# A two-layer graph network on one core: product order in layer 0, start-up, block sums and last stages changed

## The chip, the core and the metric

The kernel runs on one core of a Trainium2 chip. A core has five engines that run their own instruction queues beside each other: TensorE (PE: matrix products, written to the eight banks of PSUM), VectorE (DVE), ScalarE (ACT), GpSimd (POOL) and SyncE (SP, which here only issues DMA transfers). They wait for each other through semaphores. The metric is the device time of one execution in microseconds (us).

## What is computed

`x` has 64 graphs of 256 nodes with 512 features, `adj` is one 256x256 matrix for all of them. All is float32.

```python
def _L0_gnn_ref(x, adj, weight, bias):
    y = jnp.einsum('nm,bmd->bnd', adj, x)
    return jnp.einsum('bnd,do->bno', y, weight) + bias

def _L1_gnn_ref(x, adj, Wq, bq, Wk, bk, Wv, bv, Wo, bo):      # 8 heads of 64
    q, k, v = (x @ Wq + bq), (x @ Wk + bk), (x @ Wv + bv)     # split into heads
    scores = jnp.einsum('bqhd,bkhd->bhqk', q, k) / jnp.sqrt(jnp.float32(HD))
    scores = scores + (1.0 - adj)[None, None, :, :] * -1000000000.0
    attn = jax.nn.softmax(scores, axis=-1)
    out = jnp.einsum('bhqk,bkhd->bqhd', attn, v).reshape(b, n, d)
    return out @ Wo + bo

h = jnp.maximum(_layernorm(x, axis=-1), 0.0)
x = x + _L0_gnn_ref(h, adj, L0_gnn_weight, L0_gnn_bias)
h = jnp.maximum(_layernorm(x, axis=-1), 0.0)
x = x + _L1_gnn_ref(h, adj, ...)
```

## The kernel before

The 64 graphs go through in 32 groups (g) of two. Each large product is cut into 2x2 blocks and computed with seven block products in place of eight (a form of Strassen's method). For this, sums of blocks are made of both factors: `s1` to `s4` of a weight, `t1` to `t4` of the data. For layer 1 of the later groups the blocks are cut once more; the small sums this needs are made by `block_sums` (of weights), `block_hidden` and `block_outputs` (of data).

The order of all instructions is the order in which the program text issues them, on each engine for itself. A list with delays helps: `after(n, f)` puts work off by n ticks, and `tick()` (L322) runs what is due. The pieces of the twice cut products are issued by strings of tokens (`QK`, `VO`, `V1`, `O1`, `OL`, from L213 on), one `|` for each tick.

**Start.** `load(0)` issues the DMAs of x's first group on SyncE's queue, eight blocks; `adj` comes through ScalarE's queue. `turn_adjacency` (L374) reorders adj on ScalarE, transposes it on TensorE and copies it out. `first_ready` normalizes group 0: VectorE makes the moments, GpSimd the power -1/2, VectorE the shift `nb`, ScalarE the normalized `h`. `first_adjacency` multiplies by adj (tiles `py`). `ready(1, ...)` does the moments and `h` for group 1, whose power `rs` is made by GpSimd and whose shift `nb` by VectorE.

**Layer 0.** For each group `project` (L508) multiplies the result yT by the layer's weight in seven products of eight matmul passes each; the calls are `layer0(g, seeds)`. There are three PSUM banks: `pa` (w_a in the profile), `pb` (w_b) and `pc` (w_c). The order, with the bank and the data operand, is a11 (pa, b11), a12 (pb, b21), s2 (pa, t2), s3 (pc, t3), s1 (pa, t1), a22 (pc, t4), s4 (pa, b22). Products into pa, and a22 into pc, add to what stands there: between them VectorE reads the intermediate value (`x<-w_a`, `x<-w_c`, L821) and adds it to x. Between the products of group g the loop sets those of `adjacency(g + 1)` (tiles `py`), 0 to 2 behind each, by the tuple `(1, 1, 2, 2, 1, 0, 0)`. The t sums are made by GpSimd (L498), t1 and t2 first and t3 and t4 some ticks later. VectorE has in one queue the reads of the seven products, the moments (L42, L43) of the group just finished and of the group g + 2, the reads of the adjacency products and the 32x32 transposes of `turn` (L1006), which wait for ScalarE's `h` (L1000).

**Layer 1.** For each group and each half of the heads (qd), `score` makes the logits and ScalarE the exponentials, `key_sum` (L1209, GpSimd) adds pairs of keys, `attend` multiplies by ones (`pden`) and v (`pav`), `invert` makes the reciprocal, and `divide` writes oT. `score` subtracts the row `top` on GpSimd or VectorE in the blocks whose PSUM was not seeded. Between them stand the projections of the next group. `block_sums` of q and k are done at g = 0, of v at g = 1, of o at g = 2; for each letter of a product four sums of 128x128 are queued, on VectorE for B, F and G (not for o), else on GpSimd.

**End.** After the last scores, part of the output projection of group 30 (`O1`) is issued, then `attend(31, 1)`, the rest of `O1`, and the output projection of group 31 (`OL`). The blocks of x that are complete are written out.

Of the kernel before, what the change touches and what calls it, by code (L numbers as in the profile page):

```python
# [11 lines left out]
ALU = mybir.AluOpType  # L12
# [60 lines left out]
def general_path(tc, x, adj, w0, b0, wq, bq, wk, bk, wv, bv, wo, bo, out):  # L73
# [159 lines left out]
    "vBj x vDc vBk vDd | vEc vDe vEd vDf vCg vp11 vCi vCh vCj vEf vCk vEe vm11 vDg | vDi vDj vEf2 vDk vDh vEi vCl "  # L233
    "vEj vEg vm10 vEk | vEl0 vEl1 vEh vEl2 ")
O1 = (
    "oCi oAz oCj oCk oA0 oBz oA1 x oFa | oA2 oA3 oFb x oCa oEa oFc | oFd oB0 oEb oFe op00 oB1 x oFf oCl0 oEc oFi "
    "| oFj oCb oFg oCl1 oFk oEd oFh oCc x oCd oFl oB2 oB3 | op10 oDa op11 oG0 oDb oG1 oCe oCf | oG2 oEe oG3 oEf "
    "oDc om11 oDd oEg oCg | oDe oDi oDf oDj oEi oEh oDk oCh oEj oEk om10 oDg | oEl oDh ")
OL = (
    "oAz oCi oCj oCk oA0 oBz oA1 oA2 | oA3 oFa op00 oCa oFb oB0 oCb | oEa oCl0 oFc oFd oCc oEb oFe oCd oCl1 oFi "  # L240
    "oCe oFf oCf oFj | oFg oFk oEc oEd oFh oCg oFl oDa oB1 op10 | oB2 oB3 oDb oCh oG0 oEe op11 oDc oDd | oG1 oEf "
    "oDe oG2 oDf oG3 oDi | om11 oEg oDj oDk oEh oDg oEi om10 oEj oEk oDh | oEl ")


@with_exitstack
def kernel(
# [92 lines left out]
    def blocks_of(xt, i, k):  # L339
        return xt[32 * i:32 * i + 32, k * NT:(k + 1) * NT, :]  # L340

    def load(g):
        X[g] = xpool.tile([P, T, D], F32, tag=f"x{g % 4}", name=f"x_{g}")
        for k in range(GB):
            for i in range(NI):
                nc.sync.dma_start(blocks_of(X[g], i, k), by_block(x[g * GB + k], i))

    def quarter(xt, i, k):

# [155 lines left out]
                nc.tensor.matmul(ps[:, m, :], lhs, rhs, start=(start and m + c == 0), stop=(c == 1),  # L505
                                 skip_group_check=True)

    def project(s, halves, by_token, name, place, first, done=None, seeds=()):  # L508

        def put(ps, i, k):
            first(place(i, k), ps, i)

        def more(ps, i, k):
            o = place(i, k)
            add(o, ps, o)

        def complete(i, k):  # L520
            if done:
# [12 lines left out]
        product(pa, s, "s2", halves, "t2", by_token, start=False, stop=False)  # L534
        put(pa, 1, 0)
        yield
        pc = pc or bank([P, 2, N], f"{name}c")
        product(pc, s, "s3", halves, "t3", by_token, start=not seeds, stop=False)
        put(pc, 1, 1)
        yield  # L540
        product(pa, s, "s1", halves, "t1", by_token, start=False, stop=False)
        more(pa, 1, 1)
        complete(1, 1)
        yield
        product(pc, s, "a22", halves, "t4", by_token, start=False)
        more(pc, 1, 0)
        give(pc)
        complete(1, 0)
        yield
        product(pa, s, "s4", halves, "b22", by_token, start=False)  # L550
        put(pa, 0, 1)
        give(pa)
        complete(0, 1)
        yield
# [10 lines left out]
    def block_sums(n):  # L565

        todo = []
        for x in SMALL[n]:
            w = W[n][BLOCKS[x][0]]
            def part(i, j):  # L570
                return w[:, j, i * P:(i + 1) * P]
            s1, s2, s4 = (spare.pop(0) for _ in range(3))
            W2[n, x] = dict(a11=part(0, 0), a12=part(0, 1), a22=part(1, 1), s1=s1, s2=s2, s3=part(1, 0), s4=s4)
            eng = nc.vector if x in "BFG" and n != "o" else nc.gpsimd
            for o, p, q, op in ((s1, part(1, 0), part(1, 1), ALU.add), (s2, s1, part(0, 0), ALU.subtract),
                                (part(1, 0), part(0, 0), part(1, 0), ALU.subtract), (s4, part(0, 1), s2, ALU.subtract)):
                todo.append((eng.tensor_tensor, o, p, q, op))
        return todo
# [272 lines left out]
    def ready(g, moments_at, scales_at, relus_at, batches=1):  # L851


        xt = X[g]
        mv = small.tile([P, T, 2], F32, tag="mv", name=f"mv0_{g}")
        n = T // batches
        h = []

        def scales(i):
            part, name = mv[:, i * n:(i + 1) * n, :], f"0_{g}_{i}"  # L860
            if g == 1:
                rs = power(nc, small, mhalf, part, name)
                h.append((rs, shift(nc, small, part, rs, name)))
            else:
                h.append(norm_scales(nc, small, mhalf, part, name))
            if i == 0:
                H0[g] = act.tile([P, T, D], F32, tag="h", name=f"h_{g}", bufs=2)

        def relu(t):
            rs, nb = h[t // n]  # L870
            nc.scalar.activation(H0[g][:, t, :], xt[:, t, :], AF.Relu,  # L871
                                 bias=nb[:, t % n:t % n + 1], scale=rs[:, t % n:t % n + 1])

        for t in range(T):
# [115 lines left out]
    def layer0(g, seeds):  # L990
# [37 lines left out]
                if len(done) == 4:  # L1028
                    after(wait + 2, leave_hidden)

        yield from project(W["0"], halves, True, f"w_{g}", lambda i, k: quarter(xt, i, k), add_to, finished, seeds)


    H1T, HH, HO = {}, {}, {}
# [33 lines left out]
    def block_outputs(g, step):  # L1068
        x = OT[g][:, 2:4, :].rearrange("p c (k n j) -> p k c n j", k=GB, j=P)
        t = KEPT["o" if g < NG - 1 else "h3"]  # L1070
        both = Blocks(x, t[:, 0:2])
        last = Blocks(HO[g].all[:, 1:3].rearrange("p t c (n j) -> p t c n j", j=P), t[:, 2:4])
        if g == NG - 1:
            both.sums(nc.gpsimd)
            last.sums(nc.gpsimd)
        else:
            after(step, last.sums, nc.gpsimd)
            after(step, both.sums, nc.gpsimd)
        O2[g] = {"C": both.one(0), "E": both.one(1), "F": last.one(0), "D": last.one(1)}
# [68 lines left out]
    def score_seeds(g, qd):  # L1148
        return {cb: score_bank(g, qd, *cb, seed=maskT_f, times=1.0 / SCALE) for cb in ((0, 0), (0, 1))}

    def score(g, qd, sums=(5, 6, 7, 8), exps=(3, 4, 5, 8), masked=None, top_at=0):


        pair = [act.tile([P, GB, 2 * NT, N], F32, tag="h", name=f"a_{g}_{qd}_{c}", bufs=2) for c in range(2)]
# [4 lines left out]
        for c in range(2):  # L1159
            for b in range(GB):  # L1160
# [18 lines left out]
                    give(ps[j])  # L1179
                if not seen:  # L1180
                    if (g == NG - 1 or (g, qd) == (0, 0)) and b == 1:
                        after(2, lambda a: nc.vector.tensor_tensor(a, a, top_b, op=ALU.subtract), a)
                    elif top_at:
                        after(top_at, lambda a: nc.gpsimd.tensor_tensor(a, a, top_b, op=ALU.subtract), a)
                    else:
                        nc.gpsimd.tensor_tensor(a, a, top_b, op=ALU.subtract)  # L1186
                if exps is None:
# [23 lines left out]
    def attend(g, qd):  # L1211
# [49 lines left out]
        def divide():  # L1261
            for f in range(2):
                nc.vector.tensor_tensor(OT[g][:, 2 * qd + f, :], po[f], rden, op=ALU.mult)  # L1263
                give(po[f])
            if final:
                after(2, note)
            late = 6 if (g, qd) == (NG - 2, 1) else 4 if (g, qd) == (NG - 1, 0) else 0
            which = ("t3", "t2", "t4") if qd else ("t1",)
            if late:
                after(late, HO[g].sums, nc.gpsimd, which)  # L1270
            else:
                HO[g].sums(nc.vector if final else nc.gpsimd, which)
            if qd and g >= FIRST2:
                block_outputs(g, late + 1)

# [16 lines left out]
    for i in range(7):  # L1292
        side[20 + i].append((lambda: next(mask_steps, None),))

    turn_adjacency()
    first_ready()
    load(1)
    ready(1, (4, 4, 4, 4), (8,), (9, 9, 9, 9))
# [14 lines left out]
    for g in range(NG - 1):  # L1313
# [3 lines left out]
        if g + 2 < NG:  # L1317
            ready(g + 2, (1, 1, 1, 1), (1,), (3, 3, 3, 3) if g else (4, 4, 4, 4))
            after(4 if g else 5, feature_sums, g + 2)
            after(5 if g else 6, last_feature_sum, g + 2)  # L1320
        weighted, turned = layer0(g, seeds), adjacency(g + 1)
        for i, n in enumerate((0, 0, 1, 2, 2, 2, 0) if g == 0 else (1, 1, 2, 2, 1, 0, 0)):
            next(weighted)
# [28 lines left out]
    for g in range(NG):  # L1352
# [2 lines left out]
        if g + 2 < NG:  # L1355
            load_hidden(g + 2)
        if g == NG - 1:
            score(g, 1, (2, 3, 5, 4), (1, 2, 4, 3), top_at=3)
        else:
            score(g, 1, exps=None if g + 1 >= FIRST2 else (3, 4, 5, 8))  # L1360
        tick()
        if g == 0:
            for pool, n, tag, used in ((const, 4 * DC, "w0_sb", None), (const, 4, "w0_s1", None), (const, 4, "w0_s2", None),
# [7 lines left out]
                    first = 3 * used[1]  # L1371
                    KEPT[used[0]] = t[:, 0:first].rearrange("p (t q) j -> p t q j", q=3)
                spare.extend(t[:, i, :] for i in range(first, n))
        for n, at in (("q", 7), ("k", 16)) if g == 0 else (("v", 3),) if g == 1 else (("o", 2),) if g == 2 else ():
            for i, work in enumerate(block_sums(n)):
                after(at + i // (2 if n == "v" else 4), *work)
        if g + 1 < FIRST2:
            for which in queries_keys(g + 1):
                run(plain(g + 1, *which))
# [5 lines left out]
            run(follow(steps, QK))  # L1385
        else:
            last = follow(quartered_outputs(g - 1), O1)
            run(last, 4)
        attend(g, 1)
        if g + 1 < NG:  # L1390
            score(g + 1, 0, (5, 6, 7, 8) if g + 1 < NG - 1 else (1, 1, 1, 1), None if g + 1 >= FIRST2 else (3, 4, 5, 8))
# [79 lines left out]
```

## Time and profile before

| what | us |
|---|---|
| median of 3 runs | 2619.58 (2619.09 to 2621.03) |
| the profiled execution | 2618.1 |
| its span, first to last instruction | 2616.3 |
| TensorE busy | 2587.3 |
| stretch 0 to 52 (start, first two groups): TensorE busy | 39.89 |
| stretch 52 to 540 (layer 0): TensorE busy | 487.16 |
| stretch 540 to 1000: TensorE busy | 456.40 |
| stretch 1000 to 2480: TensorE busy | 1480.00 |
| stretch 2570 to 2616.3 (end): TensorE busy | 33.95 |

In the profile, PE is a matmul and PEld the load of its weights. A float32 matmul shows as two passes. A row of the timeline has the start, the length from the first start to the last end of the merged instructions, the engine and line, and out<-in by the program's names. The brackets at the end give the idle time of the engine before it and what ended it. Passes overlap: eight of 256 columns that follow each other take 1.73 us from start to start although each is listed with 379 ns. In the list of waits the columns are the total, the number and the longest.

### The profile page before, as it was taken

The numbers are of one execution on the slowest core, as the hardware profiler recorded it, in microseconds if no ns is written. First come the engines' busy times: TensorE is split into PE (matmuls) and PEld (weight loads), VectorE is DVE, ScalarE is ACT, GpSimd is POOL, SyncE is SP. The second block draws the span as 40 slices with busy tenths as digits, with TensorE's granted clock in tenths as the row PEclk, the third lists the DMA queues.
The fourth block names the chain that finished last, engine by engine and source line by source line (L and its number), as shares of the span: only waits on it lengthen the run. The fifth ranks groups of instructions, "written<-read, shape, count | busy, mean of one in ns | idle before, by whom it ended". The sixth has DMA issues, their size and how long they took to land.

```text
span 2616.3 us, 57383 instructions
## 1 busy us (share of the span) xinstructions
PE 2587.3 (99%) x21876; PEld 2304.1 (88%) x21876; DVE 1910.3 (73%) x4165; ACT 1379.8 (53%) x3198; POOL 2077.2 (79%) x2259
## 2 busy tenths in 40 slices
PE   8999999999999999999999999999999999999998
PEld 7999899998888888888888888888888888888886
DVE  6888788875576677777776777777777777777776
ACT  4545454543455555555555555555555555555553
POOL 6788887774788888888877888888888888887785
PEclk9999999999999999999999999999999999999999
DMA  5776666664111222211111111111122221111101
GB/s 149 198 193 182 171 165 184 161 163 112 33 50 49 64 63 66 54 50 50 50 49 50 49 50 50 50 50 49 49 62 64 65 56 50 50 49 50 50 34 50
DMA packets 281111, 211.40 MB, mean 81 GB/s; under 512 B 145920, under 2 KB 212992, under 8 KB 280832
## 3 DMA queue, kind: packets, MB, share of 16 engines
q1 hardware_dynamic: 280224, 207.02, 29.9%
q8 instruction: 175, 2.87, 0.4%
q14 instruction: 104, 0.85, 0.1%
q10 hardware_dynamic: 608, 0.66, 0.1%
HBM read 106.96 MB, written 100.66 MB: 79 GB/s over the span
## 4 chain that ended last, share of the span: by engine, by line
PE 88%; POOL 5%; DVE 4%; DMA 2%; issue 1%; SPq 1%; ACT 1%; DVEq 0%; ACTq 0%; POOLq 0%
PE sc L1166 9%; PE pav L1225 8%; PE o_pa L662 4%; PE pden L1218 2%; PE v_pa L648 2%; PE q_pa L648 2%; PE k_pa L648 2%; PE v_pa L662 2%; PE o_pc L662 2%; PE q_pa L662 2%; PE k_pa L662 2%; PE o_pa L648 2%; PE v_pc L648 1%; PE q_pc L648 1%; PE k_pc L648 1%; DVE st L42 1%
## 5 line engine op out<-in xcount | busy, mean ns | idle before, releaser
L1174 DVE SCALAR_TENSOR_TENSOR a<-sc,top 128x512 f32<-128x512 f32 x256 | 159.0, 684 | 262.1 <-PE sc L1166 262.1
L1209 POOL TENSOR_TENSOR as<-a 128x512 f32<-128x512 f32 x256 | 320.4, 1281 | 7.8 <-ACT a L1202 6.2
L1186 POOL TENSOR_TENSOR a<-a,top 128x1024 f32<-128x1024 f32 x124 | 291.1, 2370 | 36.7 <-DVE a L1177 36.7
L1242 POOL TENSOR_TENSOR as<-as 128x512 f32<-128x512 f32 x64 | 80.9, 1264 | 275.1 <-ACT as L1241 264.3
L1202 ACT ACTIVATE a<-a 128x1024 f32<-128x1024 f32 x256 | 271.9, 1063 | 23.5 <-POOL a L1186 11.9
L1166 PE MATMUL sc<-q,k 64*128 64x256 f32 x2048 | 239.5, 383 | 0.0
L1166 PEld LDWEIGHTS sc<-q,k 64*128 64x128 f32 x2048 | 196.7, 187 | 43.3 <-issue 25.4
L1225 PE MATMUL pav<-a,v 128*32 128x256 f32 x4096 | 233.6, 379 | 0.0
L1225 PEld LDWEIGHTS pav<-a,v 128*32 128x32 f32 x4096 | 133.6, 110 | 87.8
L1232 ACT ACTIVATE as<-pden 128x512 f32<-128x512 f32 x64 | 38.3, 598 | 283.3 <-PE pden L1218 283.3
L42 DVE BATCH_NORM_STATS2 st<-x 128x6 f32<-128x512 f32 x256 | 173.2, 677 | 10.8 <-DMA x<-in_x_dram 8.0
L1177 DVE SCALAR_TENSOR_TENSOR a<-sc,maskT 128x512 f32<-128x512 f32 x256 | 158.3, 681 | 0.0
L306 ACT ACTIVATE sc<-maskT 128x512 f32<-128x512 f32 x256 | 137.5, 590 | 0.0
L1000 ACT ACTIVATE h<-x,nb,rs 128x512 f32<-128x512 f32 x128 | 97.2, 808 | 65.7 <-POOL nb L54 63.9
L871 ACT ACTIVATE h<-x,nb,rs 128x512 f32<-128x512 f32 x124 | 90.8, 803 | 65.4 <-POOL nb L54 62.3
L934 POOL TENSOR_TENSOR hs<-h 128x512 f32<-128x512 f32 x31 | 39.4, 1270 | 72.9 <-ACT h L871 71.1
L821 DVE TENSOR_TENSOR x<-o_pa,x 128x512 f32<-128x512 f32 (+1 forms) x121 | 82.4, 682 | 9.0 <-PE o_pa L662 5.2
L1263 DVE TENSOR_TENSOR oT<-pav,as 128x512 f32<-128x512 f32 x128 | 82.1, 683 | 9.2 <-POOL as L1244 9.2
L1087 ACT ACTIVATE q<-q_pa,bq_c 128x256 f32<-128x256 f32 (+1 forms) x150 | 61.7, 456 | 50.1 <-PE q_pa L648 37.6
L597 POOL TENSOR_TENSOR spare<-h1T,spare 128x128 f32<-128x128 f32 x180 | 82.2, 456 | 7.0
L1244 POOL TENSOR_TENSOR as<-as 128x512 f32<-128x512 f32 x64 | 81.0, 1265 | 5.4
L498 POOL TENSOR_TENSOR t_y<-yT,t_y 128x512 f32<-128x512 f32 (+1 forms) x65 | 82.2, 1265 | 3.4 <-ACT yT L906 1.0
(1637 smaller groups left out, 8741.1 us busy)
## 6 DMA issues: line engine op xcount, KB each, us to landing
x<-in_x_dram SPq DMA_DIRECT2D x256, 128.0 KB, 3.0
residual<-x SPq DMA_DIRECT2D x256, 128.0 KB, 2.5
hidden<-r SPq DMA_DIRECT2D x128, 256.0 KB, 4.5
h1T<-hidden SPq DMA_DIRECT2D x64, 512.0 KB, 7.4
x<-residual SPq DMA_DIRECT2D x32, 1024.0 KB, 7.9
out_dram<-x SPq DMA_DIRECT2D x62, 512.0 KB, 4.1
w_sb<-in_L_gnn_weight_dram SPq DMA_DIRECT2D x1, 1024.0 KB, 8.3
wq_sb<-in_L_gnn_Wq_dram SPq DMA_DIRECT2D x1, 1024.0 KB, 7.3
```

The source lines that it names most:

```text
L42: nc.vector.bn_stats(st, src)
L306: nc.scalar.mul(t, seed, times)
L648: nc.tensor.matmul(o[:, 0, :], lhs, rhs, start=bool(fresh), stop=True, skip_group_check=True)
L662: nc.tensor.matmul(t[:, m, :], lhs, rhs, start=starts, stop=True, skip_group_check=True)
L1000: nc.scalar.activation(h1[:, k * NT + t, :], xt[:, k * NT + t, :], AF.Relu, bias=nb[:, t:t + 1], scale=rs[:, t:t + 1])
L1166: nc.tensor.matmul(ps[j][:, kt * N:(kt + 1) * N], k[j * HD:(j + 1) * HD, c, kt * P:(kt + 1) * P], q[j * HD:(j + 1) * HD, c, :], start=(kt ...
L1174: nc.vector.scalar_tensor_tensor(o, ps[j].rearrange("p (k n) -> p k n", k=NT), SCALE, top_b[:, 0:NT, :], op0=ALU.mult, op1=ALU.subtract)
L1177: nc.vector.scalar_tensor_tensor(o.rearrange("p k n -> p (k n)"), ps[j], SCALE, maskT_f, op0=ALU.mult, op1=ALU.add)
L1186: nc.gpsimd.tensor_tensor(a, a, top_b, op=ALU.subtract)
L1202: nc.scalar.activation(a, a, AF.Exp)
L1209: nc.gpsimd.tensor_tensor(AS[c, b], a4[:, :, 0, :], a4[:, :, 1, :], op=ALU.add)
L1225: nc.tensor.matmul(po[f][h * 32:(h + 1) * 32, b * N:(b + 1) * N], v[:, k, h * HD + f * 32:h * HD + f * 32 + 32], A[h // 2, b][:, (h % 2) * ...
```

## The change

It has these parts:

- `project` gets `spaced`: in layer 0 the product s1 t1 (into pa) is issued ahead of s3 t3 (into pc). The value of pa is then the first to be added to the (1,1) quarter of x, that of pc the second.
- `keep_busy`: 11 matmuls of the identity by itself, 128x128, ahead of adj's transposes on TensorE, and 8 behind them, into a bank that is given back without being read.
- two of the first four DMA blocks of x are issued on ScalarE's queue, ahead of adj's.
- `ready` makes the shift `nb` of group 1 when the first `h` is issued, and no longer together with the power; `last_feature_sum(2)` comes one tick later.
- the `block_sums` of v are all on GpSimd, from tick 9 on, eight to a tick; those of o start at tick 9 and not at 2.
- last stages: new strings `O1` and `OL`; six and not four groups of `O1` ahead of `attend(31, 1)`; the subtractions of `top` in `score(31, 1)` are no longer put off; the final sums of the data (t2, then t3, t4) on VectorE in another order; the block sums for `OL` in another order and two in separate halves.

```diff
-    def project(s, halves, by_token, name, place, first, done=None, seeds=()):
+    def project(s, halves, by_token, name, place, first, done=None, seeds=(), spaced=False):
...
-        pc = pc or bank([P, 2, N], f"{name}c")
-        product(pc, s, "s3", halves, "t3", by_token, start=not seeds, stop=False)
-        put(pc, 1, 1)
-        yield
-        product(pa, s, "s1", halves, "t1", by_token, start=False, stop=False)
-        more(pa, 1, 1)
-        complete(1, 1)
-        yield
+        def third(then):
+            nonlocal pc
+            pc = pc or bank([P, 2, N], f"{name}c")
+            product(pc, s, "s3", halves, "t3", by_token, start=not seeds, stop=False)
+            then(pc, 1, 1)
+
+        def fifth(then):
+            product(pa, s, "s1", halves, "t1", by_token, start=False, stop=False)
+            then(pa, 1, 1)
+
+        for part, then in ((fifth, put), (third, more)) if spaced else ((third, put), (fifth, more)):
+            part(then)
+            if then is more:
+                complete(1, 1)
+            yield
...
-        yield from project(W["0"], halves, True, f"w_{g}", lambda i, k: quarter(xt, i, k), add_to, finished, seeds)
+        yield from project(W["0"], halves, True, f"w_{g}", lambda i, k: quarter(xt, i, k), add_to, finished, seeds, spaced=True)
...
-                nc.sync.dma_start(blocks_of(X[g], i, k), by_block(x[g * GB + k], i))
+                queue = nc.scalar if (g, k) == (0, 0) and i % 2 else nc.sync
+                queue.dma_start(blocks_of(X[g], i, k), by_block(x[g * GB + k], i))
...
+    idle = bank([P, NT, N], "idle")
+
+    def keep_busy(n):
+
+        for _ in range(n):
+            nc.tensor.matmul(idle[:, 0, 0:P], ident, ident, start=True, stop=True)
+
+    keep_busy(11)
     turn_adjacency()
+    keep_busy(8)
+    give(idle, False)
...
             if g == 1:
-                rs = power(nc, small, mhalf, part, name)
-                h.append((rs, shift(nc, small, part, rs, name)))
+                h.append((power(nc, small, mhalf, part, name), None))
...
         def relu(t):
             rs, nb = h[t // n]
+            if nb is None:
+                nb = shift(nc, small, mv[:, t // n * n:(t // n + 1) * n, :], rs, f"0_{g}_{t // n}")
+                h[t // n] = rs, nb
...
-            eng = nc.vector if x in "BFG" and n != "o" else nc.gpsimd
+            eng = nc.vector if x in "BFG" and n in "qk" else nc.gpsimd
...
-        for n, at in (("q", 7), ("k", 16)) if g == 0 else (("v", 3),) if g == 1 else (("o", 2),) if g == 2 else ():
+        for n, at in (("q", 7), ("k", 16)) if g == 0 else (("v", 9),) if g == 1 else (("o", 9),) if g == 2 else ():
             for i, work in enumerate(block_sums(n)):
-                after(at + i // (2 if n == "v" else 4), *work)
+                after(at + i // (8 if n == "v" else 4), *work)
...
-            after(5 if g else 6, last_feature_sum, g + 2)
+            after(5 if g else 7, last_feature_sum, g + 2)
...
         if g == NG - 1:
-            both.sums(nc.gpsimd)
-            last.sums(nc.gpsimd)
+            for part in (last.one(0), last.one(1), both):
+                part.sums(nc.gpsimd)
...
-                        after(2, lambda a: nc.vector.tensor_tensor(a, a, top_b, op=ALU.subtract), a)
-                    elif top_at:
-                        after(top_at, lambda a: nc.gpsimd.tensor_tensor(a, a, top_b, op=ALU.subtract), a)
+                        after(0 if qd else 2, lambda a: nc.vector.tensor_tensor(a, a, top_b, op=ALU.subtract), a)
...
-            if late:
+            if final:
+                HO[g].sums(nc.vector, ("t2", "t3", "t4"))
+            elif late:
...
-            score(g, 1, (2, 3, 5, 4), (1, 2, 4, 3), top_at=3)
+            score(g, 1, (2, 3, 5, 4), (1, 2, 4, 3))
...
-            run(last, 4)
+            run(last, 6)
...
 O1 = (
-    "oCi oAz oCj oCk oA0 oBz oA1 x oFa | oA2 oA3 oFb x oCa oEa oFc | oFd oB0 oEb oFe op00 oB1 x oFf oCl0 oEc oFi "
+    "oAz oFa oFb oA0 oBz oFc oA1 x | oA2 oDa oCa x oEa oFd oA3 oFe oB0 | oFf oB1 x oB2 oB3 oFg op00 | oCb oEb oFi "
...
 OL = (
-    "oAz oCi oCj oCk oA0 oBz oA1 oA2 | oA3 oFa op00 oCa oFb oB0 oCb | oEa oCl0 oFc oFd oCc oEb oFe oCd oCl1 oFi "
+    "oAz oBz oA0 oA1 oA2 | oEa oA3 oFa oCi oFb oB0 oEb oB1 op00 | oB2 oFc oFd oB3 oFe oCj op11 oFf | oFi oFg oFj "
...
```

More of the change, by code (lines that the diff above doesn't have):

```diff
@@ L235 @@
 O1 = (
-    "oCi oAz oCj oCk oA0 oBz oA1 x oFa | oA2 oA3 oFb x oCa oEa oFc | oFd oB0 oEb oFe op00 oB1 x oFf oCl0 oEc oFi "
-    "| oFj oCb oFg oCl1 oFk oEd oFh oCc x oCd oFl oB2 oB3 | op10 oDa op11 oG0 oDb oG1 oCe oCf | oG2 oEe oG3 oEf "
-    "oDc om11 oDd oEg oCg | oDe oDi oDf oDj oEi oEh oDk oCh oEj oEk om10 oDg | oEl oDh ")
+    "oAz oFa oFb oA0 oBz oFc oA1 x | oA2 oDa oCa x oEa oFd oA3 oFe oB0 | oFf oB1 x oB2 oB3 oFg op00 | oCb oEb oFi "
+    "op11 oFj oFk oEc oFh x oEd | oCc oFl oCd oDi op10 oDj oDk oCi oEe oCj om10 oG0 | oG1 oEf oDb oG2 oCe oCf oG3 "
+    "oDc om11 | oDd oEg oCk oDe oCg oDf oEi oEj oCh oEk oEh oDg | oEl oDh oCl0 oCl1 ")
 OL = (
-    "oAz oCi oCj oCk oA0 oBz oA1 oA2 | oA3 oFa op00 oCa oFb oB0 oCb | oEa oCl0 oFc oFd oCc oEb oFe oCd oCl1 oFi "
-    "oCe oFf oCf oFj | oFg oFk oEc oEd oFh oCg oFl oDa oB1 op10 | oB2 oB3 oDb oCh oG0 oEe op11 oDc oDd | oG1 oEf "
-    "oDe oG2 oDf oG3 oDi | om11 oEg oDj oDk oEh oDg oEi om10 oEj oEk oDh | oEl ")
+    "oAz oBz oA0 oA1 oA2 | oEa oA3 oFa oCi oFb oB0 oEb oB1 op00 | oB2 oFc oFd oB3 oFe oCj op11 oFf | oFi oFg oFj "
+    "oFk oDi oFh oDj oFl oDk oCa oDa op10 | oDb oCb oG0 om10 oDc oDd oG1 oDe | oDf oCk oCc oCl0 oCd oG2 oCl1 oG3 "
+    "oCe oCf oDg oEc om11 | oEd oCg oDh oEi oEe oEj oEf oEk oCh oEg oEl | oEh ")
 @with_exitstack
@@ L1149, in score_seeds, with score @@
         return {cb: score_bank(g, qd, *cb, seed=maskT_f, times=1.0 / SCALE) for cb in ((0, 0), (0, 1))}
-    def score(g, qd, sums=(5, 6, 7, 8), exps=(3, 4, 5, 8), masked=None, top_at=0):
+    def score(g, qd, sums=(5, 6, 7, 8), exps=(3, 4, 5, 8), masked=None):
         pair = [act.tile([P, GB, 2 * NT, N], F32, tag="h", name=f"a_{g}_{qd}_{c}", bufs=2) for c in range(2)]
@@ L1268, in divide @@
             which = ("t3", "t2", "t4") if qd else ("t1",)
-            if late:
+            if final:
+                HO[g].sums(nc.vector, ("t2", "t3", "t4"))
+            elif late:
                 after(late, HO[g].sums, nc.gpsimd, which)
             else:
-                HO[g].sums(nc.vector if final else nc.gpsimd, which)
+                HO[g].sums(nc.gpsimd, which)
             if qd and g >= FIRST2:
```

## The prediction

> **What bounds the kernel now.** I read the page's busy shares first, then the idle waits of TensorE, then the timeline of each stretch that the diff touches. The busy shares make TensorE (PE) the bound: a change can gain only where it waits or runs slowly, and it loses where it makes TensorE wait.
>
> ```profile
> PE 2587.3 (99%) x21876; PEld 2304.1 (88%) x21876; DVE 1910.3 (73%) x4165; ACT 1379.8 (53%) x3198; POOL 2077.2 (79%) x2259
> ```
>
> The list of TensorE's waits has three places: the start, one wait in the middle, the end.
>
> ```profile
> PE pa L382 <- ACT adj_p L377: 6.5, 1, 6.5
> PE o_Fs L648 <- ACT o_F L685: 2.9, 1, 2.9
> PE py L897 <- ACT h L842: 2.8, 1, 2.8
> PE o_Es L648 <- DVE x L821: 2.8, 1, 2.8
> PE w_0a L505 <- DVE x L821: 1.7, 1, 1.7
> PE q_pb L648 <- DVE q_F L821: 1.4, 1, 1.4
> PE pden L1218 <- POOL as L1209: 1.4, 2, 0.8
> ```
>
> Layer 0 is not in that list but is what the first edit reorders in all 32 groups. One round of it, by the timeline (start, length, engine and line, out<-in):
>
> ```profile
> 207.51 1.89 PE L505 MATMUL w_9a<-w_s,yT 128*128 128x256 f32 x8
> 207.71 0.69 DVE L821 TENSOR_TENSOR x<-w_9c,x 128x512 f32<-128x512 f32 x1 [1.93 <-PE w_9c L505]
> ...
> 214.47 1.89 PE L505 MATMUL w_10a<-w_s,t_y 128*128 128x256 f32 x8
> ...
> 216.91 1.28 POOL L498 TENSOR_TENSOR yT<-yT 128x512 f32<-128x512 f32 x1
> 216.92 1.29 DVE L1006 STREAM_TRANSPOSE r<-h 128x512 f32<-128x512 f32 x2
> 217.09 1.06 PE L950 MATMUL py_11b<-adjT,h 128*128 128x128 f32 x8
> 218.14 0.65 DVE L821 TENSOR_TENSOR x<-w_10a,x 128x512 f32<-128x512 f32 x1
> ```
>
> See two things. The product s3 t3 (w_10c) starts at 218.25, when GpSimd has written t3 (216.91 + 1.28 = 218.19), about 0.25 late. And VectorE's read of bank pa after s2 t2, the last row, begins only at 218.14 and ends at 218.79, although its product ended at 216.2. VectorE is working off a queue. The windows view, from the read of the a22 product (207.71) to the end of that row, has it (columns: PE, PEld, DVE, ACT, POOL busy, clock, DMA share, GB/s):
>
> ```profile
> 207.71:218.79 11.08, 10.99 (x67) 9.93 (x66) 10.66 (x24) 4.07 (x7) 10.29 (x15) 1.00 0.75 203
> 341.01:352.10 11.09, 11.09 (x68) 10.20 (x67) 10.67 (x24) 4.65 (x7) 10.15 (x15) 1.00 0.57 153
> ```
>
> VectorE is busy for 10.66 of 11.08 us, and for the same length in a round where t3 is not late.
>
> **What the Trainium skill says.** "PSUM — Partial Sum Buffer", section "Engine vs sequencer instructions": VectorE's queue is strict first in, first out, and matmuls start in program order; the rows above agree, the finished s2 product waits its turn behind two transposes. The same page's section on bank collisions wants accesses of two engines to a bank guarded by semaphores, so the next product into pa must wait for that read. "SBUF — State Buffer", section "SBUF: two separate sides": VectorE with two SBUF inputs and GpSimd lock each other out of a shared port; the trace agrees, a 128x128 VectorE sum that takes 0.28 elsewhere took 1.72 and 2.33 from 732.69 on, beside a GpSimd pass. "TensorE: Matmul & The Clock Gate", Part 1: the array starts at half clock until a window of about 3.4 us was busy; the trace agrees, 10 passes of 128x256 in 4.42 us from 10.48, 22 in 4.40 us from 15.30.
>
> **Part 1: s1 t1 ahead of s3 t3.** Nothing is added or removed; only the order of products and of VectorE's reads changes. Before, pa is written by s2 and then by s1 3.5 us of TensorE work later (s3 and two adjacency products lie between). After, s1 follows s2 with only two adjacency products between, and those end before VectorE has read pa.
>
> Take round 10, with the end of the a22 product (207.51) as zero. TensorE is ready for the third product after s4, a11, adjacency, a12, adjacency, s2 (4 x 1.73 + 2 x 0.89 = 8.69) and two more adjacency products (1.79): 10.48. VectorE has read s2 out of pa at 218.79 - 207.51 = 11.28. From VectorE's end to a waiting product pass 0.14 us (the wait of w_31a: 605.99 to 606.13), and its first pass is 0.08 longer. So s1 starts at 11.42. In round 17 the read ends at 11.28 too, so this is VectorE's own work and not a wait that moves with TensorE. From s1 on: 1.73 + 0.08, two adjacency products 1.79, s3 1.73, one adjacency product 0.89. Then a22 goes into pc, which s3 has just filled: VectorE's read starts 0.20 after the product, lasts 0.69, plus 0.14, against 0.89 of cover: 0.14 late, and 0.08 for the first pass. Then a22 itself, 1.73. Round: 11.42 + 1.81 + 1.79 + 1.73 + 0.89 + 0.22 + 1.73 = 19.59. Before it was 18.70 where t3 was late (207.51 to 226.21) and 18.34 where it was not (322.47 to 340.81). The t3 wait is gone, and VectorE's read is late in its place.
>
> From the end of a22 in group 1 (58.62) to that in group 30 (600.45) there are 29 rounds, 541.8 us. After: 29 x 19.59 = 568.1, plus what the longer VectorE queues of some rounds (bias and mask steps: their reads of s2 ended 0.3 to 1.7 later than 11.28) and one round held by TensorE's own bias product (2.5) cost above 11.28: 8.6, the shorter last round taken off. Sum 576.7: +34.9. I take it whole because nothing in VectorE's queue moves forward. Bounds: with 0.06 us for the signal, no longer first passes and half of the extra steps hidden, +21; with all at their largest, +38.
>
> Group 1: s1 is not late there (its read ends 0.8 before TensorE is ready), a22 is: +0.2. Group 31 runs without adjacency products: s1 waits 1.1 where s3 waited 0.5, and a22 directly behind s3 waits 0.20 + 0.69 + 0.14 + 0.08 = 1.1: +1.7.
>
> **Part 2: the start.** TensorE's py products start at 10.48 and run 11 passes at half clock. 19 more small matmuls before and behind the adjacency transposes warm it; they cover TensorE's idle time and cost nothing as long as they end before h. Two of x's first four blocks go ahead of adj on ScalarE's queue: x is complete earlier (VectorE's first row started at 7.41), but adj, which ended ScalarE's wait at 5.98, is issued two DMAs later (4 issues took 1.85, so some 0.9), and ScalarE must turn adj before it makes h. I put py at 10.0, and 32 passes at 0.216 end at 16.9 instead of 19.8: 2.9. The shift of nb_1 behind x<-w_0a in VectorE's queue takes away the wait for GpSimd's power (23.16), so s2 starts at about 21.4 instead of 25.72: 4.3 ahead. What is late next: h_1, moved back with nb_1, costs the adjacency product about 0.9, and s1 of group 0 now waits for VectorE's sums of w, four moments of x_2 (26.58 to 29.8, 3.4 us, whose data come when the DMAs let them) and two reads: s1 at 27.7, s3 at 31.3, where the fourth product stood at 32.32. Gain left: 1.0. Bounds: 0, if x_2 lands no earlier, to 3.5.
>
> **Part 3: block sums of v and o.** 12 small sums of v leave VectorE; GpSimd takes 12 x 0.46 = 5.5 us more, behind the key sums, in a stretch where it was idle for 7.9 of 10 us (750 to 760). The port lock-out that held q_F until 736.71 goes with them: 1.4 and its followers 0.7 (738.5, 751.9), and the key sum that held pden at 818 comes ahead of the sums of o: 0.8. Gain 2.9 (bounds 1.5 and 3.2).
>
> **Part 4: the last stages.**
>
> ```profile
> 2570.00:2616.30 46.30, 33.95 (x252) 28.14 (x249) 29.62 (x65) 10.18 (x21) 21.54 (x23) 0.89 0.13 47
> ...
> 2578.71 0.79 PE L648 MATMUL o_Fs<-spare 128*128 128x128 f32 x2 [2.85 <-ACT o_F L685]
> ...
> 2584.54 0.84 PE L1218 MATMUL pden<-as,ones 128*32 128x256 f32 x10 [0.77 <-POOL as L1209]
> ...
> 2594.45 0.49 PE L648 MATMUL o_Es<-spare,spare 128*128 128x128 f32 x2 [2.81 <-DVE x L821]
> ```
>
> Each long wait also drops the clock (0.89). The new order gives TensorE 9.6 us of products before attend (20 of 128 columns at 0.22, 12 of 256 at 0.43) instead of 7.0, and GpSimd subtracts top first instead of idling 1.49 at 2575: its last key sum ends near 2582.7 instead of 2584.5, about when TensorE is there. Behind attend (4.3 plus 0.3 to the next read) are left 8 small O1 products, 1.8, and OL's 28 small and 12 large ones, 11.6, with about 0.8 of waits: 2582.7 + 4.6 + 14.2 = 2601.5, and 1 us more for waits I haven't found, 2602.4 against 2610.4. Gain 8.0; bounds 4 (one long wait stays) and 10.5.
>
> **The sum.** Against the profiled run (2618.1; span 2616.3): -1.0 + 0.2 + 34.9 + 1.7 - 2.9 - 8.0 = +24.9, so 2643.0. The median before is 1.5 above that run, so the forecast for a median is 2644.5.
>
> **The rivals.** (a) 72%: as summed, 2637 to 2650. (b) 12%: the read is late, but the signal is short, first passes are not longer and the extra steps are hidden, +21 for the loop; with the same other parts 2631. For it: GpSimd's signal for t3 took only 0.06. (c) 10%, faster: s1's wait for pa is covered. Then the t3 waits go (with the first pass 0.1 to 0.36 a round, 6.0 in all), no new ones come, and the sum is -1.0 - 6.0 - 2.9 - 8.0 = -17.9: 2601.7. It decides if VectorE reads s2 within 10.3 us of a22's end; 11.28 in round after round speaks against it. (d) 6%: the loop as in (a) and the end gains nothing because another wait follows the first: 2652.
>
> **The numbers.** The measurement can tell 0.2%, 5.2 us. Only (c) lies below that line: faster 10%; about 2% fall within it, slower 88%. The range 2630 to 2652 takes in (a), (b) and most of (d).
>
> **What would show it.** In layer 0: a round of 19.6, w_a<-w_s,t_y twice in a row with a wait of about 0.9 for DVE x before the second, none for t_y, and a short one before the second w_c. The start: py in passes of 0.216 from the first. The middle: no wait of q_pb. The end: clock near 1.00. I am wrong if the list of waits has no new row of w against DVE x.

## The result, and the profile after

The changed kernel takes 2642.5 us (median of 4 runs, 2641.07 to 2643.14) against 2619.66 before: 1.0086 times, with a 95% interval of 1.0068 to 1.0103. It is slower by 22.8 us; the forecast was 2644.5, range 2630 to 2652. The profiled execution has a span of 2640.4 us, 24.1 more than before.

TensorE is still the bound, but it now waits, as the page's busy shares show:

```profile
PE 2599.5 (98%) x21914; PEld 2310.3 (87%) x21914; DVE 1906.0 (72%) x4153; ACT 1385.9 (52%) x3198; POOL 2085.1 (79%) x2275
```

TensorE is busy for 12.2 us more than before (8.6 of them the small matmuls of the start, in which it had stood idle), and the rest of the 24.1 is idle time. The list of TensorE's waits in the changed kernel (line, releaser, then total, times, longest) shows where:

```profile
PE pa L383 <- ACT adj_p L378: 2.6, 1, 2.6
PE o_pb L656 <- DVE x L829: 1.9, 1, 1.9
PE w_0a L506 <- DVE x L829: 1.9, 1, 1.9
PE w_25a L506 <- DVE x L829: 1.6, 1, 1.6
...
PE o_pa L656 <- DVE x L829: 1.1, 1, 1.1
...
PE py_1a L960 <- ACT h L881: 0.7, 1, 0.7
...
PE w_10a L506 <- DVE x L829: 0.7, 1, 0.7
```

The row of w_10a stands there for nearly every group: w against DVE x, the row that the prediction asked for. Before, only groups 0 and 31 had it. The long waits of the middle and the end, `q_pb`, `pden`, `o_Fs` (2.9) and `o_Es`, are gone, and `o_pb` is new.

One round of the changed kernel by its timeline (start, length, engine and line, out<-in):

```profile
217.22 0.69 DVE L829 TENSOR_TENSOR x<-w_9c,x 128x512 f32<-128x512 f32 x1 [2.15 <-PE w_9c L506]
...
223.98 1.89 PE L506 MATMUL w_10a<-w_s,t_y 128*128 128x256 f32 x8
...
226.42 1.29 DVE L1016 STREAM_TRANSPOSE r<-h 128x512 f32<-128x512 f32 x2
...
226.60 1.06 PE L960 MATMUL py_11b<-adjT,h 128*128 128x128 f32 x8
...
227.64 0.65 DVE L829 TENSOR_TENSOR x<-w_10a,x 128x512 f32<-128x512 f32 x1
...
228.34 1.99 PE L506 MATMUL w_10a<-w_s,t_y 128*128 128x256 f32 x8 [0.69 <-DVE x L829]
...
234.73 1.97 PE L506 MATMUL w_10c<-w_sb,t_y 128*128 128x256 f32 x8
```

The second w_10a<-w_s,t_y is s1. After the adjacency product py_11b TensorE could go on at 227.49 (226.60, and 0.89 for its eight passes from start to start); VectorE ends its read of pa at 228.29, and s1 starts at 228.34. The last row is a22 (1.97 long, where 1.89 is a product that didn't wait): it starts 0.15 late, for VectorE's read of s3. The windows view of the same stretch, from the read of the a22 product to the end of the read of s2 (columns: PE, PEld, DVE, ACT, POOL busy, clock, DMA share, GB/s):

```profile
217.22:228.29 11.07, 10.43 (x64) 9.43 (x62) 10.66 (x24) 4.72 (x8) 9.39 (x17) 1.00 0.54 140
```

VectorE is busy for 10.66 of 11.07, to the hundredth what it was before. Nothing in its queue has moved; TensorE now wants the read sooner than VectorE comes to it.

Where the 24.1 us come from, by the starts of the same products in both traces:

| stretch | forecast | measured |
|---|---|---|
| start, to the first product of group 1 (41.08 to 43.74) | -1.0 | +2.7 |
| group 1 | +0.2 | -0.4 |
| 29 rounds, end of a22 in group 1 to that in group 30 (541.8 to 571.0) | +34.9 | +29.1 |
| group 31 | +1.7 | +1.6 |
| middle, up to the last stages | -2.9 | -4.1 |
| last stages | -8.0 | -4.8 |
| sum | +24.9 | +24.1 |

The sum is right within 1 us, and partly by luck: the start and the end were forecast 6.9 too good, the loop, the middle and the groups 1 and 31 7.7 too bad.

### The profile page after: what moved, and what is told of

Its sections match the earlier page's. It is cut to its first block, busy times and chain, and to the rows that moved or that the text cites. A ratio compares the mean times of both kernels' runs of the same rounds, so it can differ in the third digit from the quotient of the medians.

```text
span 2640.4 us, 57496 instructions
## 1 busy us (share of the span) xinstructions
PE 2599.5 (98%) x21914; PEld 2310.3 (87%) x21914; DVE 1906.0 (72%) x4153; ACT 1385.9 (52%) x3198; POOL 2085.1 (79%) x2275
## 4 chain that ended last, share of the span: by engine, by line
PE 86%; DVE 9%; DMA 2%; issue 1%; POOL 1%; SPq 1%; ACT 0%; DVEq 0%; POOLq 0%; ACTq 0%
PE sc L1176 9%; PE pav L1233 8%; DVE st L42 4%; PE o_pa L670 4%; DVE x L829 2%; PE pden L1226 2%; PE q_pa L656 2%; PE k_pa L656 2%; PE v_pa L656 2%; PE v_pa L670 2%; PE k_pa L670 2%; PE q_pa L670 2%; PE o_pc L670 2%; PE q_pc L656 2%; PE k_pc L656 2%; PE v_pc L656 1%
## 5 line engine op out<-in xcount | busy, mean ns | idle before, releaser
L1210 ACT ACTIVATE a<-a 128x1024 f32<-128x1024 f32 x256 | 272.4, 1065 | 18.6 <-POOL a L1194 15.7
```

Source lines behind the costliest of these rows:

```text
L1210: nc.scalar.activation(a, a, AF.Exp)
```

## The experiments

Each was timed beside runs of the kernel before on the same chip; the differences below are against those.

**1 to 4: the change taken apart.** The swap alone is the diff's edits of `project` and of its call in `layer0`, in the kernel before.

> The kernel before with s1 t1 ahead of s3 t3 and nothing else. Theory (the swap makes TensorE wait for VectorE's read of pa): rounds of 19.5 in the loop, +29 there, +1.6 in group 31, -0.4 in group 1, and about +3.5 in group 0, where s1 would stand behind the moments of x_2 in VectorE's queue: together +30 to +35, so 2650 to 2655. Rival (the loss needs the other parts, such as the later h_1 or GpSimd's new work): below +20, 2640 or less.

2652.04 us against 2618.09: +34.0, ratio 1.0128 (1.0111 to 1.0145). In its trace group 1 starts at 44.92 instead of 41.08 (+3.8), the 29 rounds take 570.9 (+29.0), group 31 +1.6. The swap alone carries the whole loss, and the loop with it is the changed kernel's round for round.

The opposite run keeps everything else:

```diff
-finished, seeds, spaced=True)
+finished, seeds)
```

> The changed kernel with s3 t3 ahead of s1 t1 again; start, block sums and last stages stay changed. Theory: the loop's rounds are those of before (18.70 and 18.34) and no w waits for VectorE in it; the middle (about -4) and the end (about -4.7) stay, and the start turns from +2.7 into a gain of 1 to 2, since s3 needs no read of VectorE: 2608 to 2611. Rival (the start is late by itself): 2614 to 2616.

2610.15, -7.9, ratio 0.9967 (0.9954 to 0.9979). No w waits for VectorE in the loop. But the start's gain is gone by the end of the loop. Group 1 ends 0.5 ahead of before, and TensorE waits for t3 from the first round on (18.69 each), where the kernel before had two rounds before that began. By the end of group 31, at 626, the kernel is 0.3 behind. These rounds are paced by GpSimd, and what TensorE gains ahead of it, it waits out in it.

The third run has the new start alone: the small matmuls, the two queues for x and the later shift of nb_1.

> The kernel before with the new start alone (small matmuls ahead, two of x's blocks on ScalarE's queue, the shift of nb_1 behind x<-w_0a). Theory: adj comes 2.5 late and the last eight small matmuls run at half clock until 13.25, so w_0a starts at 20.5 as in the changed kernel, no gain up to there; s2 starts at 24.0 instead of 25.7: the time falls by 1 to 2, 2618. Rival (the new start costs the 2.7 that the changed kernel is late at group 1): 2622.

2617.07, -1.0, ratio 0.9997 (0.9989 to 1.0006): no difference that can be told. w_0a starts at 20.27 (20.31 before), s2 at 23.82 (25.72), the first product of group 1 at 41.03 (41.08). The new start by itself neither gains nor loses; the 2.7 of the changed kernel is the swap in group 0.

The fourth has the new last stages alone (strings, top, sums, the 6 pieces ahead of attend).

> The kernel before with the new last stages alone. Theory: -4 to -5.5, as in the changed kernel, with attend's denominators about 1.5 earlier and one wait of 1.9 for VectorE (o_pb) behind it: 2614 to 2615.5. Rival (the end gains the 8 that was forecast, and what the changed kernel lacks was lost by GpSimd's later block sums): 2611 to 2612.

2614.25, -3.8, ratio 0.9985 (0.9978 to 0.9992). The denominators start at 2583.29 and the wait of 1.9 for `o_pb` is there. The rival falls: no part of the 8.0 that were forecast was lost to GpSimd's block sums.

**5: VectorE's queue made longer.** One transpose ahead of the read is done twice.

```diff
-            for t in range(NT):
+            for t in (0, 0, 1) if k == done[0] else (0, 1):
                 nc.vector.transpose(r[:, :, k, t, :], ...
```

> The changed kernel with one of VectorE's two transposes ahead of its read of s2 done twice in every round (the same data to the same place, 0.65 more in VectorE's queue). Theory (s1 waits until VectorE's queue has come to the read of pa): the wait before s1 grows from 0.85 to 1.50, the round from 19.52 to 20.17, 28 rounds times 0.65 = +18, 2660. Rival (the wait is the price of the product order or of the bank, and VectorE's queue has slack): no more than 3 slower, 2645 or less.

One run: 2666.74 against 2619.04, and a span of 2664.9 against the changed kernel's 2640.4. Its timeline of the same place:

```profile
233.67 2.04 DVE L1016 STREAM_TRANSPOSE r<-h 128x512 f32<-128x512 f32 x3
...
235.64 0.65 DVE L829 TENSOR_TENSOR x<-w_10a,x 128x512 f32<-128x512 f32 x1
...
236.34 1.99 PE L506 MATMUL w_10a<-w_s,t_y 128*128 128x256 f32 x8 [1.44 <-DVE x L829]
```

Three transposes take 2.04 where two took 1.29: 0.75 more; one of the three writes again what another wrote. The wait in front of s1 is 1.44 instead of 0.69, and a round 20.27 instead of 19.52. All of the 0.75 reaches TensorE. The span rose by 24.5 and not 18 because the addition was 0.75 (28 rounds make 21), group 25's round lost 1.6 more (its wait of 2.35 is followed by 3.4 us at half clock), and groups 1 and 31 lost 0.7 and 0.5 too.

**6: more of TensorE's work in front of s1.**

```diff
-(1, 1, 2, 2, 1, 0, 0)
+(1, 1, 3, 0, 2, 0, 0)
```

> The changed kernel, with the adjacency products dealt out 1, 1, 3, 0, 2, 0, 0 to a round in place of 1, 1, 2, 2, 1, 0, 0: three behind s2, two behind s3. Theory: s1 has 0.89 more cover and the wait of 0.85 goes, a22 too has cover for VectorE's read of s3: the round falls from 19.52 to 18.4 to 18.7 (18.34 is TensorE's own work; 18.70 was the round when GpSimd's t3 was late), so -24 to -33, 2610 to 2619. Rival (the order of the products costs by itself, whatever stands between them): within 3 of 2642.

2616.41 against 2619.04, ratio 0.9991 (0.9982 to 0.9999), so 26 below the changed kernel. The products have the changed kernel's order, and the rows of w against DVE x are gone but for groups 0, 25 and 31. Most rounds are 18.40 or 18.7. The 29 rounds take 543.7, where run 2 without the swap has 542.6. So with this cover the order costs about 1 in the loop; what stands between s2 and s1 decides.

**7: VectorE's queue shortened, first try.** Two of the four moments of the group after next go behind the read, and what follows from them goes two ticks later.

```diff
-            ready(g + 2, (1, 1, 1, 1), (1,), (3, 3, 3, 3) if g else ...)
-            after(4 if g else 5, feature_sums, g + 2)
-            after(5 if g else 7, last_feature_sum, g + 2)
+            ready(g + 2, (1, 1, 3, 3) if g else ..., (3,) if g else (1,), (5, 5, 5, 5) if g else ...)
+            after(6 if g else 5, feature_sums, g + 2)
+            after(7, last_feature_sum, g + 2)
```

> The changed kernel with two of the four moments of the group after next behind the read of s2 in VectorE's queue instead of ahead of it (their scales and what follows two ticks later). TensorE's order stays. Theory: the read of s2 comes 1.6 earlier and the wait of s1 goes; that of a22 (0.22) stays: round 18.6 to 18.7, -24 to -27, 2615 to 2619. Rival (the place in VectorE's queue doesn't matter, or its work is only moved to stand before another read): less than -8, 2634 or more.

2642.1, as the changed kernel: the rival's number. The trace shows why:

```profile
219.07 1.99 PE L506 MATMUL w_10a<-w_sb,yT 128*128 128x256 f32 x8 [0.31 <-ACT w_10a L306]
...
221.16 1.27 POOL L944 TENSOR_TENSOR hs<-h 128x512 f32<-128x512 f32 x1
...
223.74 1.27 POOL L944 TENSOR_TENSOR hs<-hs,h 128x512 f32<-128x512 f32 x1
...
223.84 1.16 PE L960 MATMUL py_11c<-adjT_t,h 128*128 128x128 f32 x8
...
228.34 1.89 PE L506 MATMUL w_10a<-w_s,t_y 128*128 128x256 f32 x8
```

s1, the last row, doesn't wait any more (1.89 long). But the first product of the group costs 0.57 (it starts 0.47 late and its first pass is 0.10 longer), behind the bias that ScalarE writes after its later `h`, and the adjacency product py_11c costs 0.42 more, waiting for the feature sums that GpSimd began only at 221.16. With a22's 0.22 that is 1.21, and the round is 18.34 + 1.21 = 19.55. The run moved too much at once to judge the theory; the next did it better.

**9: VectorE's queue shortened, without anything hanging on it.** The two transposes ahead of the read go one tick later; only a store to memory follows from them.

```diff
-                after(wait + 1, turn, k)
+                after(wait + (2 if len(done) < 4 else 1), turn, k)
```

> The changed kernel with the two transposes that stand ahead of the read of s2 in VectorE's queue put behind it (one tick later); nothing else waits for them, and GpSimd's and ScalarE's work stays where it is. Theory: the read of s2 ends at 9.99 after a22's end instead of 11.28, TensorE is there at 10.48: the wait of 0.85 and the longer first pass go, a22's 0.22 stays; round 18.57 or, where GpSimd sets the pace, 18.7: 28 rounds times 0.82 to 0.95, -23 to -27, 2616 to 2619. Rival (as in the run with the moments later, another wait takes the place): less than -8, 2634 or more.

2615.65 against 2619.74, ratio 0.9985 (0.9978 to 0.9992): 27 below the changed kernel with one line. The round is 18.56, as forecast (18.57). Its timeline:

```profile
199.63 0.68 DVE L829 TENSOR_TENSOR x<-w_9a,x 128x512 f32<-128x512 f32 x1
...
199.80 1.06 PE L960 MATMUL py_10b<-adjT,h 128*128 128x128 f32 x8
...
200.70 1.89 PE L506 MATMUL w_9a<-w_s,t_y 128*128 128x256 f32 x8
...
201.60 2.48 DVE L1016 STREAM_TRANSPOSE r<-h 128x512 f32<-128x512 f32 x4
```

The read of s2 ends at 200.31, ahead of TensorE's arrival at 200.70, and the four transposes come after it. With run 5 this shows the cause from both sides: the place of one read in VectorE's queue.

**8: the start.** All of x's first blocks go through SyncE's queue again, so adj stands first in ScalarE's.

```diff
-                queue = nc.scalar if (g, k) == (0, 0) and i % 2 else nc.sync
-                queue.dma_start(...)
+                nc.sync.dma_start(...)
```

> The changed kernel with all of x's first blocks on SyncE's queue again, so that adj stands first in ScalarE's. Theory (the start lost its gain because adj was 2.5 late and the array had cooled again): adj is turned from 6.0 on, the eight small matmuls behind it run at full clock and end near 9.4, py starts at 10.4 and its 32 passes end near 17.5 instead of 20.2; of these 2.6 some 1 to 2.6 are left at group 1: 2640 to 2641.5. Rival (adj's place doesn't matter): py at 13, 2642.5.

2642.2, no gain. Its first half came true: adj is turned from 5.80 on, the small matmuls run at full clock, w_0a starts at 17.99 instead of 20.47. The second didn't. Group 1 starts at 43.69 (43.74), because group 0's s1 waits for VectorE all the same, and TensorE's clock drops in that wait.

**10 to 12: a version that beats both.** In the kernel without the swap TensorE waits for t3 in the rounds of 18.7. The last feature sum (1.27 on GpSimd) stands ahead of t3 and is wanted only for the last adjacency product of the next round.

```diff
-            after(5 if g else 7, last_feature_sum, g + 2)
+            after(8 if g else 7, last_feature_sum, g + 2)
```

> The changed kernel without the swap, and with the last feature sum of a group (1.27 on GpSimd) behind the sums of t3 and t4 in GpSimd's queue (one round's tick 1 instead of tick 5). Theory (in the rounds of 18.70 TensorE waits for t3 because GpSimd comes to it 0.25 late): t3 is 1.27 earlier, the wait of 0.25 + 0.1 goes in some 17 rounds, and the start's small gain isn't eaten: -5 to -7 against the kernel without the swap, 2603 to 2605. Rival (the pace is set by the ring of GpSimd and ScalarE, not by t3's place): the wait moves to another product and the time stays at 2610.

2605.70 against 2619.74, ratio 0.9948 (0.9932 to 0.9965), and 4.4 below run 2, where 5 to 7 was forecast. The 29 rounds take 538.2 instead of 542.6 without it: 18.34 in most, some 18.57 in groups 8 to 12 and at the end, where GpSimd still sets the pace: in group 10 it ends t3 at 214.73, TensorE could go on at 214.66 and starts s3 at 214.79. The start happened to be 1.3 better at the end of group 1 in this execution, since adj landed about 1 us earlier in it.

> As the run before, and adj first in ScalarE's queue (x's first blocks on SyncE's alone). Theory: w_0a starts 2.5 earlier (18.0 instead of 20.4); without the swap the third product of group 0 doesn't wait for VectorE, so 1 to 2.5 of it are left at the end if GpSimd no longer sets the pace: 2601 to 2604. Rival (group 0 waits for x_2 or h_1 instead, or the loop's ring eats it): as the run before.

2605.21, ratio 0.9945 (0.9929 to 0.9962), not to be told from the run before, which was the rival's number; the first w_0a starts at 18.23. At the start of group 1 it is 1.7 ahead of run 2 and at the end of group 30 5.3, but run 10, 0.4 behind it at group 1, is 0.4 ahead by then: the loop takes 538.9 here and 538.2 there. That an earlier start is kept through the loop isn't shown. Last, the swap put back with all its waits covered:

```diff
-(1, 1, 2, 2, 1, 0, 0)
+(1, 1, 2, 1, 2, 0, 0)
-                after(wait + 1, turn, k)
+                after(wait + (2 if len(done) < 4 else 1), turn, k)
-finished, seeds)
+finished, seeds, spaced=0 < g < NG - 1)
```

> The kernel of the run before (adj first, last feature sum later), with the swap again in groups 1 to 30, but covered: the two transposes behind the read of s2, and one adjacency product moved from behind s1 to behind s3 (1, 1, 2, 1, 2, 0, 0). Theory: s1 waits no longer (read at 9.99, TensorE at 10.48), a22 has two products of cover for VectorE's read, t3 is wanted 3.5 later than GpSimd has it: rounds of 18.34 throughout, where the run before had 18.34 to 18.57: -3 to -5 against it, 2600 to 2603. Rival (GpSimd's ring sets 18.6 whatever the order): 2605, and more with every first pass that waits.

2606.28, ratio 0.9951 (0.9935 to 0.9968). Most rounds have no wait for VectorE, and 15 of the 29 take 18.34, but in groups 8 to 12 they are again 18.6. The timeline shows what is late there:

```profile
215.36 1.52 ACT L1009 ACTIVATE h<-x,nb,rs 128x512 f32<-128x512 f32 x2
...
216.78 0.57 ACT L978 COPY yT<-py_11a 128x512 f32<-128x512 f32 x1
...
217.40 1.16 PE L959 MATMUL py_11a<-adjT_t,hs 128*128 128x128 f32 x8
```

The adjacency product's bank is emptied by a copy on ScalarE, and that copy stands behind two `h` whose scales GpSimd delivers at 215.12 (the row before in its queue). TensorE was there at 217.24. The loop takes 539.3 against 538.9 in the run before. 2600 to 2603 was forecast, and the rival held: with the waits covered, the swap is worth nothing that these runs can tell, and GpSimd and ScalarE set the pace in those rounds.

## Why the prediction was right, and where it was not

**The mechanism and the loop.** Right, and shown by runs 1, 5, 6 and 9. The round was forecast at 19.59 and is 19.52 (19 of 29 are 19.51 to 19.53). Two terms of its sum were mis-sized. The signal from VectorE to TensorE was put at 0.14 and is 0.05 (228.29 to 228.34). That was the half of rival (b) that was true; its other half, first passes that don't grow, was not (0.10 longer). And the rounds with longer queues were to cost 8.6 in all and cost 5.0: six rounds lose 0.31 to 0.35, one 0.58, one 0.91, the round of the bias product 2.47, and the last one is 0.95 short. Two groups, 14 and 30, have no wait in front of s1 at all.

**Group 1 and group 31.** The wait of a22 and the two waits of group 31 (0.95 each, first passes apart) came as worked out. Group 1 came out 0.4 shorter and not 0.2 longer because its old wait for t2 (0.82) went, which the step hadn't counted. It went with the swap alone (run 1) and with the new start alone (run 3) too.

**The start.** This is the step that failed: a gain of 1.0 was forecast (bounds 0 and 3.5), and 2.7 were lost. "I put py at 10.0" was wrong by 3.1. The timeline of the changed kernel's start:

```profile
8.52 0.71 ACT L378 COPY adj_p<-adj_r 128x256 f32<-128x256 f32 x2 [6.50 <-DMA b_r<-in_L_gnn_bias_dram]
...
8.98 0.93 PE L383 MATMUL pa<-ident,adj_p 128*128 128x128 f32 x4 [2.60 <-ACT adj_p L378]
...
9.70 3.55 PE L1310 MATMUL idle<-ident 128*128 128x128 f32 x16
...
13.08 7.07 PE L907 MATMUL py<-adjT,h 128*128 128x256 f32 x32
...
29.70 3.42 PE L506 MATMUL w_0a<-w_s,t_y 128*128 128x256 f32 x8 [1.89 <-DVE x L829]
```

adj was forecast "some 0.9" later and was 2.5 later (5.98 to 8.52). (The first row names the DMA of b_r, but that landed only at 9.68; adj's last landed at 8.45.) I had counted two more issues on ScalarE, but its third and fourth DMA of adj were issued only at 3.96 and 5.20, when SyncE's stood still too: in both kernels the two queues start eight DMAs by 2.64, and the ninth comes only when the first has landed (landed 3.49, issued 3.51 before; 3.94 and 3.96 after, and the tenth at 4.34, when the second had landed at 4.33). The Trainium skill, "DMA: Bandwidth & Descriptors", section "Issuing engines are not separate DMA queues", says that DMAs of different engines run on the same 16 DMA engines and that a second issuing engine saves only the time of issuing; the trace agrees: VectorE's first row on x came 1.8 earlier (5.62 instead of 7.41), ScalarE's on adj 2.5 later. Meanwhile, after TensorE's wait of 2.60 for adj, the clock had fallen to half (9.62 to 13.03): the eight matmuls behind the transposes ran at half clock (16 passes in 3.55, against 1.95 in run 11) and stood ahead of py until 13.25, though the first h was there at 11.24. The condition that I had written, that they end before h, wasn't met. So py ran at full clock but late, and the 2.9 of gain came to nothing: in run 3 w_0a starts where it did before. What the later shift had won at s2 (1.9 in run 3) went in two steps of 0.9: the wait for h_1, which the step had counted, and the wait for GpSimd's sum of it in front of the next adjacency product, which it hadn't.

Then the swap in group 0: I had s1 at 27.7, it came at 29.70, 1.9 of it waiting, and the last row shows its 8 passes in 3.42 at half clock, where they take 1.9. Run 1 against the kernel before puts the swap's price in group 0 at 3.8, run 2 against the changed kernel at 2.6. The step had the wait, with too early an end of VectorE's list, and didn't have the clock that goes with it.

**The middle.** The waits named went, and what followed them was larger: q_pb 1.6, its followers up to 755 another 1.6 (0.7 forecast), the denominators at 818 1.1 (0.8). Some 0.5 came back later. Runs 3 and 4, without the new block sums, keep the wait of 1.4; run 2 hasn't got it. Part 3 wasn't run by itself.

**The end.** Half right. The front of it came nearly as worked out: the denominators start at 2583.29 in run 4, which was 0.4 behind up to there, instead of 2584.54, and 2582.7 was forecast. Behind attend 1.8 of waits were allowed ("0.8" and "1 us more for waits I haven't found") and there were 3.2; longer first passes and other small steps, which the sum left out, came to 0.9, and from TensorE's last product to the end it is 0.5 longer than before. (OL's products were put at 11.6; by the prices given, 28 of 0.22 and 12 of 0.43, they are 11.3.) The timeline of the changed kernel:

```profile
2618.26 1.28 DVE L1271 TENSOR_TENSOR oT<-pav,as 128x512 f32<-128x512 f32 x2
...
2619.57 0.69 DVE L499 TENSOR_TENSOR t_o<-oT,t_o 128x512 f32<-128x512 f32 x1
...
2621.65 0.68 DVE L829 TENSOR_TENSOR x<-o_pa,x 128x512 f32<-128x512 f32 x1
...
2622.25 0.41 DVE L829 TENSOR_TENSOR x<-o_Ds,x 128x256 f32<-128x256 f32 x1
...
2622.58 0.61 DVE L829 TENSOR_TENSOR x<-o_pb,x 128x256 f32<-128x256 f32 x2
...
2622.72 0.49 PE L656 MATMUL o_pb<-wo_sb,oT 128*128 128x128 f32 x2 [1.91 <-DVE x L829]
```

It is the loop's pattern again. The bank pb is full, TensorE wants to write it anew, and its read stands in VectorE's queue behind the three sums of t_o and two other reads. I looked for it in layer 0 and not here.

**The rivals.** (c), that the wait would be covered, needed the read of s2 within 10.3 of a22's end. It was 11.28 (217.01 to 228.29), the number that the kernel before had shown. Run 9 brought it to 10.1, and the wait in front of s1 went as (c) has it. The loop then took 543.7, not the 535.8 that (c) makes of 541.8: the wait of a22, 0.22 a round, stayed, and (c) had no new waits. (d) had the right doubt about the end at the wrong size.

## What to carry to other kernels

Before two products into one bank are brought closer together, add up what the reading engine has in its queue ahead of the read: the read's place in that queue, not the product's length, is when the bank comes free. If it is late, move work that nobody waits for behind the read (one line gave back 27 us here). But ask first what the new order is to gain: with its waits covered it gained nothing here (run 12). A gain ahead of a stretch that another engine paces is waited out there, so make that engine's path shorter first. And a total that comes out right within 1 us may hold three terms that are wrong by 3 to 6 each: check the terms against the trace, not the sum.

## What the runs showed of the hardware

A wait of TensorE can take its clock down. In these traces single waits of up to 1.76 us (run 5) didn't, those from 2.26 us on at full clock did, and one of 1.9 went both ways in the same program text of the last stages. The wait of 1.9 for `o_pb` left the clock at 1.00 in the changed kernel and took it down in run 4, by the windows view of the stretch behind it:

```profile
2594.50:2598.40 3.90, 3.90 (x16) 3.36 (x16) 1.83 (x8) 0.27 (x1) 3.67 (x8) 0.61 0.71 269
```

With it goes where the wait falls. In each trace the granted clock changes only at points that lie a multiple of 3.41 us apart. In run 4 one step is 2591.91 to 2595.32, the wait (2592.34 to 2594.24) lies inside it, and the next step has a clock of 0.50. In run 12 the wait (2584.82 to 2586.73) lies across the point 2586.32, and the clock stays. Of the runs with this wait, 2, 4, 9 and 10 have it inside one step and lose the clock; 5, 6, 7, 8, 11 and 12 have it across two and don't; in the changed kernel it begins at such a point (2620.81), and the clock stays too. No run here moved a wait on purpose to test this.

At the start the same program text idled 1.68 in run 11, across two steps, and py kept the full clock; in run 12 x landed 0.5 later, TensorE idled 2.26, and the clock fell 1.4 after py's start, from 12.67 to 16.09:

```profile
11.28 2.03 PE L906 MATMUL py<-adjT,h 128*128 128x256 f32 x7 [2.26 <-ACT h L849]
```

From py's first pass to its last it is 6.80 in the one and 8.48 in the other, and w_0a started at 18.23 and at 20.45. So the loss of clock cost 1.7 there, and 1.5 in group 0 of the changed kernel (8 passes of s1 in 3.42 instead of 1.9). In group 0 two waits, 0.73 and 1.89 within 3.6 us, stood ahead of it.
